# Products in 64-column halves, and seven products for eight in the third stage of a four-stage graph network

## The chip, the cores and the metric

The kernel runs on one core of a Trainium2 chip. The metric is the time of one execution on the device in microseconds (us). All data are float32.

## The reference

There are 32 graphs of 512 nodes with 128 features each, and each graph has a dense 512 x 512 weight matrix `adj`. Four residual stages follow one another; each normalises its input (layer norm and relu) and adds its result.

```python
h = relu(layernorm(x)); x = x + L0(h, adj)   # D^-1/2 (adj+I) D^-1/2 (h W) + b, leaky relu
h = relu(layernorm(x)); x = x + L1(h, adj)   # adj @ elu(.), adj^T @ elu(.), elu(.) -> W_upd, tanh
h = relu(layernorm(x)); x = x + L2(h, adj)   # four layers, see below
h = relu(layernorm(x)); x = x + L3(h, adj)   # tanh(adj @ msg), then a GRU cell
# a layer of L2; its inputs are f, f, [f, f1], [f, f1, f0] for i = 0..3
src_agg = l2norm_rows(adj)   @ (f @ ws + bs)
dst_agg = l2norm_cols(adj).T @ (f @ wd + bd)
f = tanh(concat([src_agg, f @ wn + bn, dst_agg]) @ wu + bu)
```

L2 is the "stage three" of the change, and the layers of L2 are counted from 0.

## The kernel before, in words

The host only lays out the inputs and hands over `adj` and its transpose. On the core, `program(b)` lists all operations of graph b, and every operation goes through `op(engine, us, emit, reads, writes)` with a planned duration: `t_mm`, `t_tt`, `t_act` and so on. Nothing is issued at that point. `Plan.order()` then plays the list through with these durations: each engine takes the ready operation with the earliest due time (`PERIOD` microseconds from graph to graph, less the planned work still behind it), and a tile of a limited kind waits for a slot. The kinds are PSUM banks (8) and SBUF slots of 2, 4 and 8 KB per partition, named `s2`, `s4` and `s8` (36, 5 and 10). What comes out is one fixed order per engine, in which several graphs are interleaved; it is issued as it stands, so an engine whose next operation is late waits for it. `kept_warm` puts idle products into planned gaps of TensorE.

Features are mostly held with 128 features (or 128 nodes) on the partitions and 512 columns in the free dimension. `a` and `aT` are the two forms of the matrix of a graph, four chunks of 128 x 512 each. A product is one `matmul` with 128 stationary columns (features, weights) and up to 512 moving ones; `mm` at L353 issues most of them, so that the tile names tell them apart. The profile shows two MATMUL and two LDWEIGHTS records for each.

The third stage works as follows. The squares of `a` and `aT` are summed on ScalarE, their inverse roots are made on POOL (L1077, `inv`), turned, sent to DRAM and spread over all partitions by SP (`rows`, L1088), and VectorE scales the columns of the eight chunks in place (L1096). Weights of the update are folded into the projections in `setup`. A layer then is: `paired_rows` (tile `sd`, four products of 256 columns, the bias added on VectorE at L791), one or two node products, and eight aggregation products of 512 columns, all into one PSUM bank (`ps_agg`), the tanh on ScalarE (L1136), ahead of it a sum on VectorE for layers 2 and 3 (L1135). Layer 1 is in `fifteen`: the two aggregations of the features themselves (eight products of 512 columns, `ps_agg<-aT,f1r` and `ps_agg<-a,f1r`), then fifteen products of 256 columns (L914) that serve layers 1, 2 and 3. The projection of layer 3 is in `seven` (L835): a two by two product of blocks in seven products, of 14 matmuls of 128 columns, with sums and differences on VectorE (L813).

Layer norms go through VectorE (`bn_stats`, L646), a power on POOL (L688, `sc`), `nb` on VectorE (L696), and four activations on ScalarE (L700, `h`). Transposes are made by VectorE in 32 x 32 blocks and a way through DRAM (`turned`, about a thousand transfers by SP), except in graphs 0, 1 and 31 (`at_ends`), where TensorE transposes 128 x 128 blocks (L733, L753, L876). POOL issues no transfers.

Of the kernel before, what the change touches and what calls it, by code (L numbers as in the profile page):

```python
# [18 lines left out]
P = 128  # L19
# [5 lines left out]
PERIOD = 37.0  # L25
# [6 lines left out]
GATES = 5 * D  # L32
FIFTEEN = GATES + 4 * D
T_COLS = FIFTEEN + 6 * D
# [65 lines left out]
class Plan:  # L100
# [65 lines left out]
    def lag(self, o, n):  # L166

        queued = o.engine == n.engine and o.engine in self.RESULT
        if queued:
            return o.us + self.RESULT[o.engine]  # L170
        return o.us + o.land + self.SIGNAL[o.engine] + self.LOAD * (n.engine == "PE")
# [110 lines left out]
def gnn_stack(  # L282
# [16 lines left out]
    plan = Plan(sb, psum, {"bank": 8, "s2": 36, "s4": 5, "s8": 10}, {"bank": 0, "s2": 4, "s4": 0, "s8": 0})  # L299
# [51 lines left out]

    def mm(ps, out_of, lhs, rhs, n, start, stop, reads, later=0.0):
        op("PE", t_mm(n), lambda: nc.tensor.matmul(out_of(ps.ap()), lhs(), rhs(), start=start, stop=stop),  # L353
           reads, [ps], later=later)

    LAST = [W_L2[3][0] + (2 * k + o) * D for k in (2, 0) for o in range(2)]
# [8 lines left out]
    def t15(k):  # L365
        return t_sb[:, FIFTEEN + k * D:FIFTEEN + (k + 1) * D]

    def setup():
# [35 lines left out]
        for i, (k, (proj, upd)) in enumerate(zip(L2_CHUNKS, RAW_L2, strict=True)):  # L404
            part = [0, 2] * k + [1] * k
            buf = raws[i][0]
            for lo in range(0, 3 * k, NC):
                n = min(NC, 3 * k - lo)
                ps = plan.bank(f"fold{i}_{lo}")
                for j in range(n):  # L410
                    mm(ps, lambda t, j=j: t[:, j * D:(j + 1) * D],
                       lambda i=i, c=proj + (lo + j) * D: block(i, c),
                       lambda i=i, c=upd + part[lo + j] * D: block(i, c), D, True, True, [buf])
                at = W_L2[i][0] + lo * D
                op("ACT", t_act(n * D), lambda ps=ps, n=n, at=at: nc.scalar.copy(
                    w_sb[:, at:at + n * D], ps.ap()[:, :n * D]), [ps], [(W2F, {i})])
# [16 lines left out]
            else:  # L433
                op("ACT", t_act(2 * D), lambda ps=ps, r=ROW_OF[i]: nc.scalar.copy(
                    rf_sb[:, r * 2 * D:(r + 1) * 2 * D], ps.ap()[:, :2 * D]), [ps], [RF])
        for at, (b11, b12, b21, b22), wbuf in ((0, LAST, (W2F, {3})), (GATES, BOTH, W3)):

# [10 lines left out]
        m, c = rf_sb, ROW_OF[3] * 2 * D  # L448
        op("DVE", t_tt(D), lambda: nc.vector.tensor_sub(t_sb[:, 4 * D:5 * D], m[:, c:c + D], m[:, c + D:c + 2 * D]), [RF], [(TS, {4})])
# [33 lines left out]
    def program(b):  # L483
# [13 lines left out]
        def gates(h3T, mT):  # L497
# [17 lines left out]
            def product(o, data, weight, wbuf, first):  # L515
                op("PE", t_mm(H), lambda: nc.tensor.matmul(o[0](), weight(), data[0](), start=first, stop=True, skip_group_check=True), [data[1], wbuf], [o[1]])  # L516

# [209 lines left out]
        def added_rows(x, m, quiet=False):  # L727

            o = buf("s2", rows_shape, "xr")
            if at_ends:  # L730
                ps = plan.bank("t")
                for c in range(NC):
                    op("PE", 0.109, lambda c=c: nc.tensor.transpose(ps.ap()[:, c * P:(c + 1) * P], m.ap()[:, c * P:(c + 1) * P], ident),  # L733
                       [m, ID], [(ps, {c})])
# [14 lines left out]
        def transposed(h, name):  # L749
            if at_ends:  # L750
                ps, hT = plan.bank("t"), buf("s2", name=name)
                for c in range(NC):
                    op("PE", 0.109, lambda c=c: nc.tensor.transpose(ps.ap()[:, c * P:(c + 1) * P], h.ap()[:, c, :], ident),  # L753
                       [(h, {c}), ID], [(ps, {c})])
# [24 lines left out]
        def paired_rows(nodes, wcols, wbuf, bias, bbuf, col):  # L779

            sd = buf("s4", (P, NC, 2 * D), "sd")
            for h in range(NC // 2):
                ps = plan.bank("sd")
                for j in range(2):
                    c = 2 * h + j
                    for k, nk in enumerate(nodes):
                        mm(ps, lambda t, j=j: t[:, j * 2 * D:(j + 1) * 2 * D],
                           lambda nk=nk, c=c: nk.ap()[:, c * P:(c + 1) * P],
                           lambda k=k: wt(wcols + k * 2 * D, 2 * D), 2 * D, k == 0, k == len(nodes) - 1, [nk, wbuf])
                part = (sd, set(range(4 * h, 4 * h + 4)))  # L790
                op("DVE", t_tt(N), lambda ps=ps, h=h: nc.vector.tensor_add(  # L791
                    sd.ap()[:, 2 * h:2 * h + 2, :], ps.ap().rearrange("p (j v) -> p j v", j=2),
                    along(bias, col, 2 * D, 2)), [ps, bbuf], [part])
            return sd

        def seven(x1, x2, dst, part, behind):

            at = 0  # L800
            (b11, b12, b21, b22), wbuf, (bias, bc), bbuf = LAST, (W2F, {3}), (rf_sb, ROW_OF[3] * 2 * D), RF
            H = N // 2
            s13, s24, ev, dv, xx = (buf("s2", (P, 2, H), k) for k in ("s13", "s24", "ev", "dv", "xx"))
            bank_a, bank_b, bank_c, bank_d = (plan.bank("seven") for _ in range(4))

            def half(m, k):
                return m.ap()[:, k * H:(k + 1) * H]

            def t(k):
                return t_sb[:, at + k * D:at + (k + 1) * D]  # L810

            def dve(o, a, b, reads, writes, sub=False, behind=()):
                op("DVE", t_tt(H), lambda: nc.vector.tensor_tensor(o(), a(), b(), op=ALU.subtract if sub else ALU.add), reads, writes, behind=behind)  # L813

            def place(k, o):
                return lambda: dst(k, o)

            def of(m, k):
                return lambda: m.ap()[:, k, :]

            def flat2(m, k):
                return lambda: m.ap()[:, k, :].rearrange("p (j v) -> p j v", j=2)

            def region(ps, k):
                return lambda: ps.ap()[:, k * H:(k + 1) * H]

            def region2(ps, k):
                return lambda: ps.ap()[:, k * H:(k + 1) * H].rearrange("p (j v) -> p j v", j=2)

            def along2(m, c):  # L830
                return lambda: m[:, None, c:c + D].to_broadcast([P, 2, D])

            def product(ps, k, lhs, rhs, reads, behind=()):
                for j in range(2):
                    op("PE", t_mm(D), lambda j=j: nc.tensor.matmul(  # L835
                        ps.ap()[:, k * H + j * D:k * H + (j + 1) * D], lhs()[:, j * P:(j + 1) * P], rhs(),
                        start=True, stop=True), reads, [ps], behind=behind)

            def pair(m):
                return lambda: m.ap().rearrange("p k (j v) -> p k j v", j=2)  # L840


            dve(of(s13, 1), lambda: half(x1, 0), lambda: half(x1, 1), [x1], [(s13, {1})], True, behind)
            product(bank_a, 0, lambda: half(x1, 0), lambda: wt(b11), [x1, wbuf], behind)
            product(bank_a, 1, of(s13, 1), lambda: t(2), [(s13, {1}), (TS, {at + 2})])
            dve(flat2(ev, 0), region2(bank_a, 0), along2(bias, bc + D), [bank_a, bbuf], [(ev, {0})])
            dve(of(ev, 1), region(bank_a, 1), of(ev, 0), [bank_a, (ev, {0})], [(ev, {1})])
            op("DVE", t_tt(N), lambda: nc.vector.tensor_add(
                pair(dv)(), pair(ev)(), t_sb[:, None, None, at + 4 * D:at + 5 * D].to_broadcast([P, 2, 2, D])), [ev, (TS, {at + 4})], [dv])

            product(bank_d, 0, lambda: half(x2, 0), lambda: wt(b21), [x2, wbuf])
            dve(of(s24, 0), lambda: half(x2, 1), of(s13, 1), [x2, (s13, {1})], [(s24, {0})], sub=True)
            dve(of(s13, 0), lambda: half(x1, 1), lambda: half(x2, 1), [x1, x2], [(s13, {0})])
            dve(of(s24, 1), lambda: half(x2, 0), of(s24, 0), [x2, (s24, {0})], [(s24, {1})], sub=True)
            product(bank_b, 0, of(s24, 0), lambda: t(1), [(s24, {0}), (TS, {at + 1})])
            product(bank_b, 1, of(s13, 0), lambda: t(0), [(s13, {0}), (TS, {at})])

            product(bank_c, 0, lambda: half(x2, 1), lambda: t(3), [x2, (TS, {at + 3}), bank_b])
            product(bank_c, 1, of(s24, 1), lambda: wt(b22), [(s24, {1}), wbuf])
            dve(place(0, 0), region2(bank_d, 0), flat2(dv, 0), [bank_d, dv], [part(0, 0)])  # L860
            op("DVE", t_tt(N), lambda: nc.vector.tensor_add(
                ev.ap(), bank_b.ap()[:, None, :H].to_broadcast([P, 2, H]), ev.ap()), [bank_b, ev], [ev])
            dve(of(xx, 0), region(bank_b, 0), of(dv, 1), [bank_b, dv], [(xx, {0})])
            dve(place(1, 1), region2(bank_b, 1), flat2(ev, 1), [bank_b, ev], [part(1, 1)])
            dve(place(1, 0), region2(bank_c, 0), flat2(xx, 0), [bank_c, (xx, {0})], [part(1, 0)])
            dve(of(xx, 1), region(bank_b, 1), of(ev, 0), [bank_b, ev], [(xx, {1})])
            dve(place(0, 1), region2(bank_c, 1), flat2(xx, 1), [bank_c, (xx, {1})], [part(0, 1)])

        def fifteen(f1, shares):


            H = N // 2
            if at_ends:
                pst, f1r = plan.bank("t"), buf("s2", rows_shape, "f1r")
                for c in range(NC):
                    op("PE", 0.109, lambda c=c: nc.tensor.transpose(pst.ap()[:, c * P:(c + 1) * P], f1.ap()[:, c * P:(c + 1) * P], ident),  # L876
                       [f1, ID], [(pst, {c})])
# [343 lines left out]
```

## Time and profile before

| what | value |
|---|---|
| time, median of 3 runs | 2275.66 us (2275.64 to 2276.08) |
| profiled execution: its time and span | 2275.95 us and 2274.2 us |
| granted TensorE clock | 1.0 |
| share of the span in which PE, PEld, DVE, ACT, POOL are busy | 100%, 58%, 71%, 48%, 10% |
| matmul records | 7608 |
| DMA: moved, mean rate, share of 16 engines of the main queue | 263.03 MB, 116 GB/s, 37.6% |

PE is TensorE's matmuls, PEld its weight loads, DVE is VectorE, ACT ScalarE, POOL GpSimd and SP SyncE, which here issues transfers. A busy time is the union of the instructions of an engine; matmuls overlap their successors, so for TensorE the distance from start to start says more than the length of a record. In a group of instructions the columns after the bar are busy time in us, mean length in ns, and the idle time of the engine just before.

### The profile page before, as it was taken

The page shows a single profiled execution, that of the slowest core. Times are in us where ns is not written, and L with a number is a line of the kernel's source. Part 1 is how long each engine was busy: PE and PEld are TensorE (multiplying, and loading weights), DVE is VectorE, ACT ScalarE, POOL GpSimd, SP SyncE. Part 2 cuts the span into 40 slices and gives each one's busy share as a digit, 9 for nine tenths or more (in the row PEclk, how much of TensorE's full clock was granted, in tenths as well). Part 3 has the DMA queues.
Part 4 walks back from the last instruction along what each step waited for, and adds up shares of the span by engine and source line. Part 5 has one row for each costly group of instructions (what it writes and reads, how often), then busy time and mean ns, then how long its engine had stood idle before and what let it go on. Part 6 is the DMA issues. An engine that isn't in the chain of part 4 may idle for free.

```text
span 2274.2 us, 25755 instructions
## 1 busy us (share of the span) xinstructions
PE 2263.3 (100%) x7608; PEld 1311.8 (58%) x7608; DVE 1607.0 (71%) x4346; ACT 1101.4 (48%) x2563; POOL 216.6 (10%) x203
## 2 busy tenths in 40 slices
PE   9999999999999999999999999999999999999999
PEld 6555565555565555555555655555555556555556
DVE  6756676767777777767777777777677777776655
ACT  7643554544445544455544455445555444552422
POOL 2100100100100100001001001000010010010000
PEclk9999999999999999999999999999999999999999
DMA  8032333444333443334443334443344333333212
GB/s 295 29 105 77 111 99 117 139 128 127 119 105 121 130 130 120 107 117 135 132 123 121 104 120 130 130 120 108 115 136 134 122 117 106 121 99 91 79 42 65
DMA packets 199052, 263.03 MB, mean 116 GB/s; under 512 B 25984, under 2 KB 130688, under 8 KB 198912
## 3 DMA queue, kind: packets, MB, share of 16 engines
q1 hardware_dynamic: 198624, 261.26, 37.6%
q8 instruction: 60, 0.98, 0.2%
q14 instruction: 80, 0.66, 0.1%
q10 hardware_dynamic: 288, 0.13, 0.0%
HBM read 199.18 MB, written 62.13 MB: 115 GB/s over the span
## 4 chain that ended last, share of the span: by engine, by line
PE 95%; DMA 2%; DVE 2%; ACT 0%; issue 0%; SPq 0%; POOL 0%; ACTq 0%; DVEq 0%; POOLq 0%
PE ps_agg L353 61%; PE ps_fifteen L914 9%; PE ps_sd L353 7%; PE ps_seven L835 4%; PE ps_seven L516 4%; PE ps_upd L353 3%; PE ps_gate L353 3%; PE ps_lin L353 1%; PE ps_msg L353 1%; PE ps_node L353 1%; DMA last<-turn_last 0%; DMA turned<-turn_turned 0%; DMA bounce<-invT 0%; DMA r_sb<-in_brow 0%; DMA turn_turned<-blk 0%; DMA rows<-bounce 0%
## 5 line engine op out<-in xcount | busy, mean ns | idle before, releaser
L353 PE MATMUL ps_agg<-a,sd 128*128 128x512 f32 x768 | 385.3, 593 | 0.0
L353 PE MATMUL ps_agg<-aT,sd 128*128 128x512 f32 x768 | 380.5, 593 | 0.4 <-DVE sd L791 0.2
L688 POOL TENSOR_TENSOR sc<-v,neg_half 128x4 f32<-128x4 f32 (+1 forms) x127 | 150.6, 1186 | 1710.5 <-DVE v L649 1603.5
L353 PEld LDWEIGHTS ps_agg<-aT,sd 128*128 128x128 f32 x768 | 136.6, 191 | 86.4 <-issue 77.5
L700 ACT ACTIVATE h<-xr,nb,sc 128x128 f32<-128x128 f32 x384 | 157.9, 482 | 49.1 <-DVE nb L696 49.1
L353 PEld LDWEIGHTS ps_agg<-a,sd 128*128 128x128 f32 x768 | 137.0, 191 | 62.0 <-issue 53.8
L353 PE MATMUL ps_sd<-w_sb,f 128*128 128x256 f32 x512 | 145.6, 380 | 0.9 <-ACT f L1112 0.9
L353 PEld LDWEIGHTS ps_sd<-w_sb,f 128*128 128x128 f32 x512 | 94.4, 190 | 77.6 <-issue 61.7
L1136 ACT ACTIVATE f<-c,cf_sb 128x512 f32<-128x512 f32 x64 | 46.2, 722 | 179.8 <-DVE c L1135 179.8
L353 PE MATMUL ps_agg<-f,w_sb 128*128 128x512 f32 x256 | 130.9, 593 | 0.1
L353 PE MATMUL ps_agg<-aT,f1r 128*128 128x512 f32 x256 | 130.7, 592 | 0.0
L353 PE MATMUL ps_agg<-a,f1r 128*128 128x512 f32 x256 | 130.7, 592 | 0.0
L353 PE MATMUL ps_agg<-aT,h 128*128 128x512 f32 (+2 forms) x260 | 128.7, 583 | 0.6 <-ACT h L673 0.6
L353 PE MATMUL ps_agg<-a,rep 128*128 128x512 f32 x256 | 125.5, 592 | 0.0
L353 PE MATMUL ps_agg<-aT,rep 128*128 128x512 f32 x256 | 121.6, 595 | 2.0 <-DVE rep L1049 1.8
L353 PE MATMUL ps_agg<-aT,msg 128*128 128x512 f32 (+1 forms) x264 | 116.7, 579 | 0.0
L791 DVE TENSOR_TENSOR sd<-ps_sd,rf_sb 128x512 f32<-128x512 f32 x128 | 87.9, 687 | 32.3 <-PE ps_sd L353 31.9
L1096 DVE TENSOR_TENSOR a<-a,rows 128x512 f32<-128x512 f32 x128 | 87.2, 687 | 16.7 <-PE ps_agg L353 16.1
L709 DVE STREAM_TRANSPOSE blk<-h 128x512 f32<-128x512 f32 x87 | 61.4, 706 | 51.4 <-ACT h L700 51.2
L1077 POOL TENSOR_TENSOR inv<-stat,neg_half 128x8 f32<-128x8 f32 x32 | 59.4, 1857 | 308.8 <-DVE stat L1076 287.9
L1096 DVE TENSOR_TENSOR aT<-aT,rows 128x512 f32<-128x512 f32 x128 | 86.4, 684 | 2.0 <-PE ps_agg L353 1.9
L1136 ACT ACTIVATE f<-ps_agg,cf_sb 128x512 f32<-128x512 f32 x32 | 22.0, 687 | 131.8 <-PE ps_agg L353 131.8
(229 smaller groups left out, 4424.6 us busy)
## 6 DMA issues: line engine op xcount, KB each, us to landing
aT<-in_adjt SPq DMA_DIRECT2D x124, 512.0 KB, 3.9
turn_turned<-blk SPq DMA_DIRECT2D x696, 64.0 KB, 1.8
turned<-turn_turned SPq DMA_DIRECT2D x174, 256.0 KB, 2.7
a<-in_adj SPq DMA_DIRECT2D x62, 512.0 KB, 7.5
rows<-bounce SPq DMA_DIRECT2D x32, 512.0 KB, 3.7
shares<-bounce SPq DMA_DIRECT2D x32, 512.0 KB, 4.4
x<-in_x SPq DMA_DIRECT2D x32, 256.0 KB, 2.7
out<-xr SPq DMA_DIRECT2D x31, 256.0 KB, 3.1
```

The costliest lines, as they stand in the source:

```text
L353: op("PE", t_mm(n), lambda: nc.tensor.matmul(out_of(ps.ap()), lhs(), rhs(), start=start, stop=stop), reads, [ps], later=later)
L516: op("PE", t_mm(H), lambda: nc.tensor.matmul(o[0](), weight(), data[0](), start=first, stop=True, skip_group_check=True), [data[1], wbuf], ...
L688: op("POOL", t_pow(n), lambda: nc.gpsimd.tensor_tensor(inv.ap()[:, :n], v8.ap()[:, :n], neg_half[:, :n], op=ALU.pow), [v8, NH], [(inv, {0})])
L700: op("ACT", t_act(D, 2), lambda c=c: nc.scalar.activation(h.ap()[:, c, :], xin.ap()[:, c, :], AF.Relu, bias=nb.ap()[:, c:c + 1], scale=inv ...
L709: op("DVE", t_tt(N), lambda: nc.vector.transpose(blk.ap().rearrange("p b (c r) -> p c b r", c=NC), m.ap().rearrange("p c (b s) -> p c b s" ...
L791: op("DVE", t_tt(N), lambda ps=ps, h=h: nc.vector.tensor_add(sd.ap()[:, 2 * h:2 * h + 2, :], ps.ap().rearrange("p (j v) -> p j v", j=2), a ...
L835: op("PE", t_mm(D), lambda j=j: nc.tensor.matmul(ps.ap()[:, k * H + j * D:k * H + (j + 1) * D], lhs()[:, j * P:(j + 1) * P], rhs(), start= ...
L914: op("PE", t_mm(H), lambda: nc.tensor.matmul(o[0](), weight(), data[0](), start=first, stop=True, skip_group_check=True), [data[1], wbuf], ...
L1077: roots = op("POOL", t_pow(2 * NC) + 0.4, lambda: nc.gpsimd.tensor_tensor(inv.ap()[:, :2 * NC], stat.ap(), neg_half, op=ALU.pow), [stat, N ...
L1096: op("DVE", t_tt(N), lambda m=m, c=c, s=s: nc.vector.tensor_mul(m.ap()[:, c, :], m.ap()[:, c, :], rows.ap()[:, s, :]), [(m, {c}), rows], [ ...
L1136: end = op("ACT", t_act(N, 1), lambda to=to, i=i, f_new=f_new: nc.scalar.activation(f_new.ap(), to.ap(), AF.Tanh, bias=cf_sb[:, i:i + 1]), ...
```

## The change

There are three parts. Every matmul of the kernel is issued as two, one for each half of the stationary columns, which write partitions 0 to 63 and 64 to 127 of PSUM (`by_halves`); the transposes on TensorE at the ends become products with the identity. In stage three the aggregations of layers 0, 2 and 3 (`features`) and of layer 1 (`edges`) are cut into two by two blocks: 64 features, two chunks of nodes, 256 columns. They take seven block products instead of eight, and two block products that write different halves of the partitions are issued side by side (`side_by_side`), each 256 columns wide. The sums of the blocks of the features are made on VectorE (`left_sums`), those of the matrices by copies on ScalarE and by transfers that POOL issues and that add to what is at their destination (`made_of`). `seven` is gone; layer 3 uses `paired_rows` with two inputs. Every second chunk of the scaled matrices, and of the projected features, has its sign turned. The weights of the projections and of the nodes are rearranged to match in `setup`.

The constants of the plan change too: `PERIOD`, the slots of `s2` and `s8`, and a new kind `s6` for the sums.

```diff
-PERIOD = 37.0
+PERIOD = 41.0
-    plan = Plan(sb, psum, {"bank": 8, "s2": 36, "s4": 5, "s8": 10}, {"bank": 0, "s2": 4, "s4": 0, "s8": 0})
+    plan = Plan(sb, psum, {"bank": 8, "s2": 31, "s4": 5, "s6": 4, "s8": 8}, {"bank": 0, "s2": 2, "s4": 0, "s6": 0, "s8": 0})
...
+    def by_halves(to, weight, data, start, stop):
+        for c in HALVES:
+            nc.tensor.matmul(to[c], weight[:, c], data, start=start, stop=stop, skip_group_check=True)
+
     def mm(ps, out_of, lhs, rhs, n, start, stop, reads, later=0.0):
-        op("PE", t_mm(n), lambda: nc.tensor.matmul(out_of(ps.ap()), lhs(), rhs(), start=start, stop=stop),
-           reads, [ps], later=later)
+        op("PE", t_mm(n), lambda: by_halves(out_of(ps.ap()), lhs(), rhs(), start, stop), reads, [ps], later=later)
+
+    def turn_on_pe(ps, part, columns, reads):
+        op("PE", t_mm(P), lambda: by_halves(ps.ap()[:, part * P:(part + 1) * P], columns(), ident, True, True), reads + [ID], [(ps, {part})])
...
-                    op("PE", 0.109, lambda c=c: nc.tensor.transpose(ps.ap()[:, c * P:(c + 1) * P], h.ap()[:, c, :], ident),
-                       [(h, {c}), ID], [(ps, {c})])
+                    turn_on_pe(ps, c, lambda c=c: h.ap()[:, c, :], [(h, {c})])
...
+        def made_of(m):
+            tm, even, odd = buf("s6", (P, 2, 3, H), "made"), {0, 2}, {1, 3}
...
+            def copied(k, src, reads):
+                op("ACT", t_act(N), lambda: nc.scalar.copy(t(k)(), src()), reads, [(tm, {k})])
+
+            def sent(o, x, reads, writes):
+                op("POOL", 1.95, lambda: nc.gpsimd.dma_start(o(), x(), accum_op=ALU.add), reads, writes).land = 5.5
+
+            copied(1, two(m, 0, 1), [(m, even)])
+            copied(0, two(m, 1, 1), [(m, odd)])
+            copied(2, two(m, 1, 0), [(m, odd)])
+            sent(two(m, 0, 1), two(m, 0, 0), [(m, even)], [(m, even)])
+            sent(t(1), two(m, 1, 1), [(m, odd), (tm, {1})], [(tm, {1})])
+            sent(t(0), two(m, 0, 1), [(m, even), (tm, {0})], [(tm, {0})])
+            sent(t(2), t(0), [(tm, {0, 2})], [(tm, {2})])
...
+        def side_by_side(lo, hi, begun):
+            for pair in zip(lo, hi, strict=True):
...
+                def emit(emits=emits):
+                    for to, lhs, rhs, start in emits:
+                        nc.tensor.matmul(to(), lhs(), rhs(), start=start, stop=True, skip_group_check=True)
+                op("PE", t_mm(H), emit, reads, writes)
+
+        def features(i, sd, nodes, made, f_new, more):
...
+            left_sums(H, lambda h, k: lambda: sd.ap().rearrange("p (q k) (h v) -> p q k h v", k=2, h=2)[:, :, k, h, :],
...
+            lo = products(A, 1, q4) + products(C, 5, q4) + node(C, 1, 1) + products(A, 2, q4) + node(A, 0, 0) + products(C, 3, q2)
+            hi = products(Bh, 6, q4) + node(Dh, 2, 1) + products(Dh, 3, (2, 3)) + products(Bh, 7, q4)
+            second = len(hi)
+            hi += products(Bh, 4, q4) + node(Bh, 1, 0)
...
+            side_by_side(lo[:4], hi[:4], begun)
+            copy(p1_lo, A)
+            add(d, p1_lo, Bh)
...
+            side_by_side(lo[4:second], hi[4:second], begun)
...
+            add(quarter[1, 1], e, C)
+            side_by_side(lo[second:], hi[second:], begun)
...
+        def edges(f1r, made, ge):
...
+            left_sums(P, part, f1r, st, lambda k: lambda: st.ap()[:, k])
...
+            products(0, 1)
...
-            ge = buf("s4", (P, 2, N), "ge")
-            for k, m in enumerate((aT, a)):
-                ps = plan.bank("agg")
-                for c in range(NC):
-                    mm(ps, lambda t: t, lambda c=c: chunk(c), lambda c=c, m=m: m.ap()[:, c, :], N, c == 0, c == NC - 1, [f1r, (m, {c})])
+            ge = buf("s4", (P, 2, N), "ge")
+            edges(f1r, made, ge)
...
-            if i == 3:
-                sd = buf("s4", (P, NC, 2 * D), "sd")
-                seven(f0, f, *of_halves(sd), [third_started])
+            if i == 3:
+                sd = paired_rows([f0, f], [wsd + 4 * D, wsd], (W2F, {i}), rf_sb, RF, ROW_OF[i] * 2 * D)
+                nodes.append((f0, wn + 2 * D, 3))
+            end = features(i, sd, nodes, made, f_new, later[i - 2] if i > 1 else None)
```

The sums of the results in `features` (`add`, `copy` and the tanh) run on VectorE and ScalarE: for layer 0 six sums of 256 columns and one copy, for layers 2 and 3 eight sums of 256, one of 512 and two copies each; in `edges` two sums and six more, all of 256, and three copies.

## The prediction

> **What bounds the kernel now.** I read the page first: the busy line and the chain of waits.
>
> ```profile
> PE 2263.3 (100%) x7608; PEld 1311.8 (58%) x7608; DVE 1607.0 (71%) x4346; ACT 1101.4 (48%) x2563; POOL 216.6 (10%) x203
> PE 95%; DMA 2%; DVE 2%; ACT 0%; issue 0%; SPq 0%; POOL 0%; ACTq 0%; DVEq 0%; POOLq 0%
> ```
>
> TensorE is busy for the whole span and 95% of the chain lies on it. A busy PE is not yet a PE at its rate, so next I read the chain in order of time, where each piece runs from start to start.
>
> ```profile
> 335.49 10.30 PE ps_agg L353 x24
> 404.87 10.30 PE ps_agg L353 x24
> 474.24 10.30 PE ps_agg L353 x24
> ...
> 2163.97 1.73 PE ps_fifteen L914 x8
> ...
> 2207.42 0.89 PE ps_seven L835 x8
> ```
>
> Two records make one float32 product, so a product takes 10.30/12 = 0.858 us with 512 moving columns, 1.73/4 = 0.4325 with 256 and 0.89/4 = 0.2225 with 128. The same run of twelve comes back every 69.37 us: that is the time of one graph. The groups by shape give the number of products (records / 2 / 32 graphs).
>
> ```profile
> L353 PE MATMUL ps_agg<-a,sd 128*128 128x512 f32 x768 | 385.3, 593 | 0.0
> L353 PE MATMUL ps_agg<-aT,sd 128*128 128x512 f32 x768 | 380.5, 593 | 0.4 <-DVE sd L791 0.2
> ...
> L353 PE MATMUL ps_agg<-f,w_sb 128*128 128x512 f32 x256 | 130.9, 593 | 0.1
> L353 PE MATMUL ps_agg<-aT,f1r 128*128 128x512 f32 x256 | 130.7, 592 | 0.0
> L353 PE MATMUL ps_agg<-a,f1r 128*128 128x512 f32 x256 | 130.7, 592 | 0.0
> ...
> L835 PE MATMUL ps_seven<-t_sb,s 128*128 128x128 f32 x384 | 63.2, 274 | 0.0
> ```
>
> Over all groups a graph has 58 products of 512, 34 of 256 and 22 of 128 columns: 58 x 0.858 + 34 x 0.4325 + 22 x 0.2225 = 69.4 us, the whole period. No engine but TensorE sets it: a column less streamed is time saved, as long as nothing else becomes late. The next engine is VectorE.
>
> ```profile
> 900.00:969.60 69.60, 69.60 (x230) 40.05 (x229) 50.84 (x139) 34.34 (x80) 6.62 (x6) 1.00 0.40 126
> ```
>
> That window (PE, PEld, DVE, ACT, POOL, clock, DMA share, GB/s) is one graph: DVE 50.8 us of 69.6, ACT 34.3, POOL 6.6.
>
> **What the Trainium skill says.** "TensorEngine Tiling (Array Packing)", Key Properties: a matmul of at most 64 stationary columns uses a column tile, tiles load weights and multiply in parallel, and a change of the tiling mode drains the array. No run here has a column tile; with every product halved there is no change of mode. "TensorE: Matmul & The Clock Gate", LDWEIGHTS: a load takes columns/1.2 ns, 107 ns for 128. The trace agrees: six loads in a row start 22.24 - 21.57 = 0.67 us apart in all, 0.112 each.
>
> ```profile
> 21.57 0.75 PEld L353 LDWEIGHTS ps_foldb<-c_sb,raw 128*128 128x128 f32 x6
> 22.24 0.19 PEld L353 LDWEIGHTS ps_foldb<-raw,c_sb 128*128 128x128 f32 x1
> ```
>
> "SBUF — State Buffer", Who interferes with whom: descriptors of a transfer issued by GpSimd wait while VectorE is in a two-port mode; no transfer is issued there before, so no trace shows it.
>
> **The change part by part.** *Halves.* Each product becomes two of 64 stationary columns, on the same 512, 256 or 128 moving columns. I take the pair at the price of one whole product: two different tiles, and 4 loads of 64 columns (an estimate of 53 ns each from the page) instead of 2 of 128, the same load time. The bounds are a little below nothing (what a product takes beyond its columns, 2 x 0.4325 - 0.858 = 0.007 us, if tiles hide it: under 1 us a graph) and twice the time (no overlap).
>
> *Seven for eight.* Layers 0, 2 and 3 of stage three had 8 aggregation products of 512 each and 1, 1 and 2 node products, 28 in all; they become 14 pairs of 256 each and two pairs for each node input: 16, 16 and 18. The two aggregations of layer 1 (8 of 512) become 14 pairs of 256. Layer 3's projection, `seven` (14 of 128), becomes 8 of 256. Before: 36 x 0.858 + 14 x 0.2225 = 34.0 us. After: (50 + 14 + 8) x 0.4325 = 31.1 us. The saving is 2.86 us a graph, **91.5 us** over 32, all of it on the path; the graph is then 66.5 us of TensorE. At both ends 80 transposes, 0.108 us each from start to start (25.03 to 25.46 for four), become identity products of 0.2225: **+9 us**, in stretches where TensorE is also full.
>
> *VectorE.* Its rate is read from start to start:
>
> ```profile
> 1103.20 0.69 DVE L1096 TENSOR_TENSOR a<-a,rows 128x512 f32<-128x512 f32 x1
> 1103.80 0.69 DVE L1096 TENSOR_TENSOR aT<-aT,rows 128x512 f32<-128x512 f32 x1
> ...
> 1115.07 0.42 DVE L908 TENSOR_TENSOR xy<-xy,ge 128x256 f32<-128x256 f32 x1
> 1115.53 0.42 DVE L908 TENSOR_TENSOR xy<-xy,f 128x256 f32<-128x256 f32 x1
> 1115.87 0.42 DVE L908 TENSOR_TENSOR q<-ge 128x256 f32<-128x256 f32 x1
> ```
>
> 0.60 us for 512 columns, 0.34 for 256 (0.46 where it needs the one before it), 0.20 for 128 as an estimate on that line. Removed: 12 of 256 and 2 of 512 in `seven`, the two sums of L1135 and four biased copies, all of 512: 12 x 0.34 + 8 x 0.60 = 8.9 us. Added: 12 biased copies, 12 left sums, 22 sums of results (6, 8, 8) and 8 in layer 1, all of 256, two of 512, four of 128, one small: 54 x 0.34 + 2 x 0.60 + 4 x 0.20 + 0.1 = 20.5 us. Net +11.6, so 62.4 us a graph; at the full lengths (0.69, 0.42, 0.28), as where each needs the last, +14.7 and 65.5. VectorE goes from 73% of the period to 94% or more of 66.5 us. Its idle 18.8 us a graph were what let it answer at once; with 1 to 4 left, TensorE will wait for sums now and then. No row prices this. Bounds: nothing, and 2.86 us a graph, at which the gain is gone (beyond it lies a rival below). I take a third, 1 us a graph: **+32 us**.
>
> *ScalarE.* Six copies of 512 (0.62 each), five more of 256 (0.37) in the layers and the tanh of layer 0 in three parts (+1.0), layer 1 +0.6: about +7 us, 41 of 66.5. Cost nothing, hidden beside TensorE; the copies come long before use, as shown next.
>
> *Transfers that add.* Eight a graph of 256 KB, issued by POOL, in two chains of up to three. "DMA: Bandwidth & Descriptors", Anatomy of one DMA, prices one at 2.0 us + bytes/436e3, 2.6 us as an estimate, and says nothing of adding; the plan books 1.95 us on POOL and 5.5 to land. A chain of three so takes 8 to 22 us. The cover: a graph's matrices are scaled until 1110.4 (the last L1096 at 1109.70), and its first features are back from DRAM only at 1136.68, its first projection at 1138.37: 28 us. So nothing on the path while the landing stays under some 8 us; past that, layer 0 waits and another graph's products must fill in. POOL rises from 6.6 to about 22 us a graph. Behind a send that waits for the one before stand the powers of L688 and L1077; the nb of L696 on VectorE, the h on ScalarE and a transpose wait for those. The DMA share of 0.40 gains 2 MB beside 8.2 (263 MB / 32), under 0.2 even if each byte counts twice: room. SP's queue issues what it did.
>
> *Buffers.* Of the 8 KB slots 8 are left of 10. A matrix lives about 270 us (issued near 967, last used near 1237), so two take 270 x 2 / 69.4 = 7.8 slots, with the reloaded one on top: the loads must come later. They are some 50 us ahead of the first use (the diagonal copy at 1017.1), so I cost this at nothing; with the cover gone, a load's 3.9 to 7.5 us would stand ahead of a graph's start. The 2 KB slots fall from 36 to 31, where `seven` alone held five. The other constants of the plan only change order.
>
> **The sum.** The profiled execution took 2275.95 us (span 2274.2, so 1.75 around it; 0.3 over the median of 2275.66): 2275.95 - 91.5 + 9 + 32 = 2225.5, said as **2226 us**.
>
> **The rivals.** *VectorE takes over as the bound (slower).* Place: the six sums behind each pair of banks, in order, with 62.4 to 65.5 us of work. If it can be kept busy only 92% of the time, the period is 65.5 / 0.92 = 71.2 us: +1.8 x 32 + 9 = 2343 us. It decides below 65.5 / 69.1 = 95% (69.1 = 69.37 - 9/32). For it: the 73% leave no precedent, and its order is fixed from planned durations. Against: the 62.4, and three to four graphs under way for TensorE to turn to.
>
> *Loads set the pace (slower).* A load of 64 columns might take as long as one of 128: 4 x 0.112 = 0.448 us a product against 0.4325 and 0.2225. That adds 106 x 0.0155 + 8 x 0.2255 = 3.45 us a graph: 2226 + 110 = 2336 us. It eats the whole saving from about 0.105 us a load. Against: the page's columns/1.2.
>
> *The halves don't overlap: the change doesn't do what it says.* Each product at twice its time: 133 us a graph, 2275.95 + 32 x (133 - 69.37) = 4312 us. For it: no column tile in this trace. Against: the skill ("TensorE: Matmul & The Clock Gate", Part 3, three column tiles ran 2.38 times as fast, though not said for float32).
>
> **How the numbers follow.** Forecast 0.55, its own range 2175 to 2265 (waits of 0 to 2.2 us a graph, and a little for overheads that tiles hide); VectorE 0.22, 2250 to 2360, a fifth of it still faster; loads 0.12, 2300 to 2420; no overlap 0.08; below 2175 0.03. A range of 2175 to 2360 holds about eight in ten. Faster 0.55 + 0.03 + 0.05 = 0.63; same 0.04; slower 0.33, where 0.2% is about what a measurement of this kernel can tell from no change.
>
> **What would show it.** Right: the pairs of one bank 0.43 us from start to start; the period near 67.5 us; DVE over 60 us a graph; TensorE's gaps short and ended by DVE sums; the sends landing in under 8 us. Wrong: products of 256 columns at 0.448 or more (loads) or 0.86 (no overlap); PE under 96% with DVE near 100%; gaps ended by a DMA of `made` or by POOL's powers, the landing or the queue I costed at nothing.

## The result and the profile after

The changed kernel takes **2499.6 us** (median of 4 runs, 2495.1 to 2502.0) where the kernel before takes 2275.9 beside it: 1.098 times as long, 95% interval 1.0961 to 1.0999. The forecast was 2226. The page of after, busy line and chain of waits:

```profile
PE 2311.3 (92%) x18376; PEld 1369.1 (55%) x18376; DVE 2025.3 (81%) x5657; ACT 1298.7 (52%) x3105; POOL 529.5 (21%) x459
PE 35%; DVE 26%; DMA 17%; issue 10%; ACT 5%; POOL 4%; SPq 2%; ACTq 0%; DVEq 0%; POOLq 0%
```

TensorE, 100% busy and 95% of the chain before, now idles 8% of the span and is a third of the chain. VectorE is no bound either; 17% of the chain are transfers, which were 2%. The queues of the DMA engines in after (packets, MB, share of all 16 engines' time):

```profile
q1 hardware_dynamic: 198624, 261.26, 35.2%
q0 software_dynamic: 69632, 67.13, 17.7%
```

The second line is new. Its 67 MB are a quarter of the other queue's bytes and take half of its time. The timeline of TensorE in after, at the same place of two neighbouring graphs (start, length, group, and in brackets the idle time before it and what ended that):

```profile
1009.30 0.65 PE L356 MATMUL ps_fifteen<-xy,w_sb 128*64 128x256 f32 x4 [2.72 <-DVE yx L1066]
...
1015.51 1.09 PE L356 MATMUL ps_msg<-w_sb,hT 128*64 128x128 f32 x16 [1.87 <-ACT hT L779]
...
1085.86 0.65 PE L356 MATMUL ps_fifteen<-xy,w_sb 128*64 128x256 f32 x4 [3.62 <-DVE yx L1066]
1086.34 1.02 PE L356 MATMUL ps_fifteen<-xy,t_sb 128*64 128x256 f32 x4
1087.14 0.64 PE L356 MATMUL ps_lin<-w_sb,agg 128*64 128x128 f32 x4
```

The period is 76.6 us here (1085.86 - 1009.30), where before had 69.37. TensorE stops for microseconds in stage three's layer 1 (`fifteen`), for a sum of VectorE. What VectorE did meanwhile, from its timeline in after:

```profile
1005.20 0.42 DVE L1066 TENSOR_TENSOR xy<-xy,f 128x256 f32<-128x256 f32 x1
1008.22 0.69 DVE L760 TENSOR_TENSOR xr<-turned,xr 128x512 f32<-128x512 f32 x1 [2.60 <-DMA turned<-turn_turned]
1008.83 0.42 DVE L1066 TENSOR_TENSOR yx<-ps_fifteen,pe 128x256 f32<-128x256 f32 x1
```

It waited 2.6 us for a turned block on its way back from DRAM, and the sum that TensorE needs came behind that. Over the whole run, the waits of VectorE for turned blocks in after (us in total, times, longest):

```profile
DVE xr L760 <- DMA turned<-turn_turned: 134.3, 56, 6.0
```

and in before:

```profile
DVE xr L738 <- DMA turned<-turn_turned: 27.6, 33, 3.9
```

The largest of TensorE's own waits in after is the one seen in the timeline:

```profile
PE ps_fifteen L356 <- DVE yx L1066: 76.5, 26, 5.8
```

The chain of after in order of time says what else is long:

```profile
992.29 9.67 DMA a<-in_adj
...
1005.28 2.92 DMA turned<-turn_turned
```

This matrix load takes 9.67 us, and the 13 loads on the chain take 9.1 to 10.1. A chain picks long transfers, so this is no fair comparison with the middle value before, 7.5 us.

A measure used below is the **late starts** of a kernel. I walk through TensorE's records from 400 to 2100 us, give each its length from start to start (a pair of halves 0.858, 0.4325 or 0.2225 us, as the prediction read them), and add up by how much they begin later than that asks for. It is 3 us for before and about 220 for after. The lengths are those at the full clock, so a product that runs at a lower clock makes the next one late too. The same lengths times all records give TensorE's work in the whole run: 2251.5 us before, 2179.0 after. The forecast's 91.5 - 9 = 82.5 us of saved work are there, less 10 us for 46 more warming products a run (`ps_idle`) that the order puts into gaps. The saved work is real; the late starts swallow it and more.

### The profile page after: what moved, and what is told of

Same layout as the page of the kernel before. It is cut to its first block, busy times and chain, and to the rows that moved or that the text cites. A ratio compares the mean times of both kernels' runs of the same rounds, so it can differ in the third digit from the quotient of the medians.

```text
span 2499.7 us, 50580 instructions
## 1 busy us (share of the span) xinstructions
PE 2311.3 (92%) x18376; PEld 1369.1 (55%) x18376; DVE 2025.3 (81%) x5657; ACT 1298.7 (52%) x3105; POOL 529.5 (21%) x459
## 3 DMA queue, kind: packets, MB, share of 16 engines
q0 software_dynamic: 69632, 67.13, 17.7%
## 4 chain that ended last, share of the span: by engine, by line
PE 35%; DVE 26%; DMA 17%; issue 10%; ACT 5%; POOL 4%; SPq 2%; ACTq 0%; DVEq 0%; POOLq 0%
PE ps_ab L892 9%; PE ps_sd L356 6%; DMA turned<-turn_turned 6%; PE ps_agg L356 5%; DMA a<-in_adj 5%; PE ps_cd L892 5%; DMA turn_turned<-blk 5%; POOL sc L711 4%; DVE blk L732 3%; DVE c L833 3%; PE ps_fifteen L356 3%; PE ps_seven L356 2%; SPq L741 2%; ACT h L723 2%; DVE bn L669 1%
## 5 line engine op out<-in xcount | busy, mean ns | idle before, releaser
L892 PE MATMUL ps_ab<-made,st 128*64 128x256 f32 x1536 | 390.3, 380 | 0.3 <-DVE p L833 0.2
L356 PE MATMUL ps_sd<-w_sb,f 128*64 128x256 f32 x2048 | 272.1, 388 | 26.1 <-DVE sd L819 13.7
L892 PE MATMUL ps_ab<-aT,sd 128*64 128x256 f32 x768 | 228.6, 385 | 1.3 <-DVE c L833 1.1
L892 PE MATMUL ps_ab<-a,sd 128*64 128x256 f32 x768 | 224.3, 380 | 0.0
L892 PEld LDWEIGHTS ps_ab<-made,st 128*64 128x64 f32 x1536 | 206.4, 137 | 25.2 <-DVE p L833 6.7
L356 PEld LDWEIGHTS ps_sd<-w_sb,f 128*64 128x64 f32 x2048 | 155.8, 140 | 110.7 <-PE ps_ab L892 23.4
L892 PE MATMUL ps_cd<-aT,st 128*64 128x256 f32 x768 | 216.1, 381 | 0.2
L892 PE MATMUL ps_cd<-a,st 128*64 128x256 f32 x768 | 210.7, 379 | 0.0
L892 PE MATMUL ps_ab<-made,sd 128*64 128x256 f32 x768 | 206.5, 386 | 0.0
L356 PE MATMUL ps_agg<-a,rep 128*64 128x512 f32 x512 | 177.5, 592 | 0.0
L760 DVE TENSOR_TENSOR xr<-turned,xr 128x512 f32<-128x512 f32 x58 | 40.1, 692 | 134.4 <-DMA turned<-turn_turned 134.3
```

What stands on the lines that cost most here:

```text
L356: nc.tensor.matmul(to[c], weight[:, c], data, start=start, stop=stop, skip_group_check=True)
L760: tt(o, lambda: nc.vector.tensor_add(o.ap().rearrange("p c (a r) -> p c a r", a=NC), turned_cols(t), x.ap().rearrange("p c (a r) -> p c a ...
L892: nc.tensor.matmul(to(), lhs(), rhs(), start=start, stop=True, skip_group_check=True)
```

## The experiments

The causes to tell apart are (1) the adding transfers, by their data and landing (1a) or by POOL's time to issue them (1b); (2) the fewer slots; (3) VectorE, by its load or by its chains of sums. Times stand beside a run of before on the same chip (2272 to 2276 us), ratios have 95% intervals.

### Halves alone

```diff
-        op("PE", t_mm(n), lambda: nc.tensor.matmul(out_of(ps.ap()), lhs(), rhs(), ...
+        op("PE", t_mm(n), lambda: by_halves(out_of(ps.ap()), lhs(), rhs(), start, stop), ...
```

> The kernel before, with every product issued as two halves of 64 stationary columns and the 80 transposes at the ends as products, and nothing else. If the halves are free, 2276 + 9 = about 2285 us. If column tiles cost something in the long run (loads, issue), 2340 us and up.

Measured 2277.6 us, ratio 1.0029 (1.0018 to 1.0040): +5.6 us, the transposes as products included. The timeline of TensorE in this kernel:

```profile
1000.81 1.03 PE L356 MATMUL ps_agg<-a,sd 128*64 128x512 f32 x4
1001.67 0.60 PE L356 MATMUL ps_fifteen<-ge,w_sb 128*64 128x256 f32 x4
1002.10 0.60 PE L356 MATMUL ps_seven<-hT,w_sb 128*64 128x256 f32 x4
```

Four half records, one pair, take 0.86 us with 512 columns and 0.43 with 256, as the whole products did. Halves cost nothing.

### After without the adding transfers

```diff
-            sent(two(m, 0, 1), two(m, 0, 0), [(m, even)], [(m, even)])
-            ... (all four of a matrix)
```

> The changed kernel without its eight adding transfers a graph (the sums of the matrices are left out, their copies on ScalarE, all sums on VectorE and the slots stay). Theory 1, the adding transfers delay the other transfers and POOL: most of the loss goes, 2230 to 2320 us. Theory 2, fewer slots make the loads late: 2430 us or more stays. Theory 3, VectorE has too much work: 2430 us or more stays.

Measured 2314.2 us, ratio 1.0185 (1.0170 to 1.0200). Without the transfers, and with a new order, 185 us are gone; it is still no gain.

### Before with the transfers, and before with the slots

```diff
+            sent(spare_t(0), two(m, 0, 0), [(m, {0, 2})], [(SPARE, {0})])
+            ... (four a matrix, into a tile that nobody reads)
```

> The kernel before, with eight adding transfers a graph of the same size and in the same chains put on POOL after the scaling, into a spare tile that nobody reads (33 slots of 2 KB for 36, to make room). Theory 1: 2350 to 2500 us. Theories 2 and 3: 2276 to 2290 us.

Measured 2365.2 us, ratio 1.0409 (1.0394 to 1.0425): 93 us although no product waits for the sums. The order is a new one here, with three slots of 2 KB fewer; what these two cost was not measured apart.

```diff
-PERIOD = 37.0
+PERIOD = 41.0
...
-"s2": 36, "s4": 5, "s8": 10}
+"s2": 31, "s4": 5, "s8": 8}
```

> The kernel before with the slots of the changed one (31 of 2 KB, 8 of 8 KB) and its PERIOD of 41, and nothing else. Theory 2: 2350 us or more, with ScalarE waiting for the loads of a. Theories 1 and 3: 2276 to 2300 us.

Measured 2312.1 us, ratio 1.0171 (1.0148 to 1.0194): the slots and the other period together cost before 40 us. It was neither the 2350 us of theory 2 nor the 2276 to 2300 of the others.

### Thin transfers

```diff
-nc.gpsimd.dma_start(o(), x(), accum_op=ALU.add)
+nc.gpsimd.dma_start(o()[:8], x()[:8], accum_op=ALU.add)
```

> The changed kernel with the same order on every engine and the same eight adding transfers and waits, but each moves the first 8 of 128 partitions only (so most of the sums of the matrices are left out). Theory 1a, what costs is the data that the adding transfers move through the DMA engines and their long landing: most of the 185 us goes, 2310 to 2350 us. Theory 1b, what costs is that POOL issues them in its queue, 1.2 us each, with powers behind: 2430 us or more.

Measured 2305.6 us, ratio 1.0138 (1.0123 to 1.0153). Order, instructions and POOL's queue are those of after, only the data are fewer, and **194 us** are gone. That is 1a and not 1b: POOL still issues all 256 transfers, though in less time (it is busy for 444.3 us in place of 529.5). VectorE's waits for turned blocks fall below those of before (12.8 us in 24 waits), the period is 70.1 us, the late starts are 85 us. TensorE's wait for `yx` is gone too:

```profile
PE ps_fifteen L356 <- DVE yx L1066: 3.1, 5, 1.2
```

A rival remains, which the prediction had named: a transfer that waits for the one before it holds up POOL's queue, and the powers of the layer norms stand behind it. VectorE's waits for these powers settle it, in after and in thin_sends:

```profile
DVE nb L719 <- POOL sc L711: 33.1, 31, 1.2
```

```profile
DVE nb L719 <- POOL sc L711: 32.7, 29, 1.2
```

They are the same, and none is longer than 1.2 us.

### The sums on GpSimd

```diff
-            sent(t(1), two(m, 1, 1), [(m, odd), (tm, {1})], [(tm, {1})])
+            sum_on("POOL", t(1), two(m, 0, 1), two(m, 1, 1), [m], [(tm, {1})])
```

> The changed kernel with the sums of the matrices made by GpSimd itself, four tensor additions of 512 columns for each matrix, straight into the tile; no adding transfers and no copies on ScalarE. Theory 1a: 2250 to 2330 us, as without the transfers. A rival, GpSimd's additions read the memory that VectorE's two-input sums read and slow them: VectorE's sums get longer and the time stays over 2350 us.

Measured 2465.9 us, ratio 1.0841 (1.0825 to 1.0857): no transfers, no copies on ScalarE, and hardly better. VectorE's groups in this kernel:

```profile
L1201 DVE TENSOR_TENSOR node<-zn,en 128x512 f32<-128x512 f32 x32 | 48.5, 1517 | 0.1
L1200 DVE TENSOR_SCALAR en<-en 128x512 f32<-128x512 f32 x32 | 40.2, 1256 | 1.3 <-ACT en L1197 1.3
L817 DVE TENSOR_TENSOR sd<-ps_sd,rf_sb 128x256 f32<-128x256 f32 x192 | 78.2, 407 | 51.7 <-PE ps_sd L356 51.7
```

and the same three in after:

```profile
L1200 DVE TENSOR_TENSOR node<-zn,en 128x512 f32<-128x512 f32 x32 | 21.8, 683 | 0.0
L1199 DVE TENSOR_SCALAR en<-en 128x512 f32<-128x512 f32 x32 | 13.4, 419 | 0.0
L817 DVE TENSOR_TENSOR sd<-ps_sd,rf_sb 128x256 f32<-128x256 f32 x192 | 78.6, 409 | 60.3 <-PE ps_sd L356 60.0
```

`node` and `en`, from SBUF to SBUF, take 1517 and 1256 ns in place of 683 and 419; `sd`, which reads one input from PSUM, takes what it took. VectorE's busy time rises by 147 us (2172.6 for 2025.3). The Trainium skill's "SBUF — State Buffer", Who interferes with whom, says so of `node`: VectorE shares a pair of ports with GpSimd, and an operation with both inputs in SBUF contends with one of GpSimd that reads SBUF. The late starts are 195 us; the largest group of them, 91, is in layer 1 (`ps_b`).

### Slots back, and fewer sums on VectorE

`no_sends_slots` gives the version without transfers its slots back ("s2" 33, "s8" 10); its products read the matrix in place of the sums.

```diff
-"s2": 31, "s4": 5, "s6": 4, "s8": 8}
+"s2": 33, "s4": 5, "s8": 10}
...
-                return (lambda: tm.ap()[:, pair, j, :]), (tm, {j})
+                return (lambda: m.ap()[:, c, h * H:(h + 1) * H]), (m, {c})
```

> The changed kernel without adding transfers, whose products read the matrix itself instead of the sums (left out), the copies going to one spare tile; the room goes back to slots: 33 of 2 KB and 10 of 8 KB. Theory 2 for the rest of the loss, too few slots: 2314 falls to 2200 to 2260 us. Theory 3, VectorE: 2300 us or more stays.

Measured 2329.9 us, ratio 1.0247 (1.0230 to 1.0264), not under 2314: more slots gain nothing there, so theory 2 doesn't explain what is left. (The order is a new one, and all graphs' copies go to one tile, so what slots alone are worth there was not measured.)

`no_left` keeps the order of after and doesn't issue the 16 left sums a graph.

```diff
-            summed(n, place(0), part(1, 1), part(1, 0), ALU.subtract, of(), [(st, {0})])
-            ... (four lines)
+                op("DVE", us, lambda: None, reads, writes)
```

> The changed kernel in the same order, with the 16 left sums a graph on VectorE not issued (the products read the blocks themselves, so these sums are left out), 4.9 us a graph less of VectorE. Theory 3, VectorE has too much work: 2350 to 2430 us. Theory 1: 2460 us or more, since the transfers stay.

Measured 2503.9 us, ratio 1.1008 (1.0992 to 1.1024): 140 us less of VectorE (1885.7), and no faster.

`thin_no_left` makes both edits, this one and the thin transfers'.

> The kernel after in its own order, with two things left out: the adding transfers move 8 of 128 partitions, and the 16 left sums a graph on VectorE (4.9 us a graph) are not issued. It asks what the thin transfers left over: they take 2306 us, and between 400 and 2100 us TensorE's products begin in all 85 us later than their lengths ask for, 3.5 us a graph. Theory A, VectorE's load: with 90% of its time taken it answers late, so with 4.9 us less a graph the waits fall to 1 us a graph and the time to about 2306 - 2.5 x 32 = 2226 us. Theory B, the length of the chains of sums and the order alone: the time stays within 12 us of 2306. The left sums alone changed nothing with the whole transfers (2504 against 2500), where late transfers ended the waits.

Measured 2304.3 us, ratio 1.0136 (1.0118 to 1.0154). VectorE's share of the stretch from 800 to 1200 us is 83% (333.8 of 400) where it was 90%, the late starts are 85 us as in thin_sends. Less load on VectorE brings nothing, with whole transfers or with thin ones.

### How the transfers cost

`unread`: in the order of after, all transfers with all bytes, and no product reads what they make.

```diff
-                return (lambda: tm.ap()[:, pair, j, :]), (tm, {j})
+                return (lambda: m.ap()[:, c, h * H:(h + 1) * H]), (tm, {j})
```

> The kernel after in its own order. All eight adding transfers are issued with all their bytes, but no product reads what they make: the products read the matrix itself instead of the sums (so the sums are left out of the result), and the transfer that adds within the matrix adds into a spare tile. Theory 1, traffic: the transfers slow the loads and the turning transfers, and these hold up the queues: the time stays within 30 us of 2500. Theory 2, lateness of the sums themselves: products wait for transfers that land late, so without that wait it falls towards the thin transfers' 2306, under 2360. Between them both have a share.

Measured 2516.0 us, ratio 1.1064 (1.1038 to 1.1090). No product waits for the sums, and the time is that of after or a little over: it is the traffic, not the lateness of the sums.

`half_sends`: 64 of 128 partitions.

```diff
-nc.gpsimd.dma_start(o(), x(), accum_op=ALU.add)
+nc.gpsimd.dma_start(o()[:64], x()[:64], accum_op=ALU.add)
```

> The kernel after in its own order, the adding transfers moving 64 of 128 partitions (the other half of each sum is left out). With 8 partitions it took 2306 us, with 128 it took 2500. If the cost goes with the bytes it is 2306 + 194 x 56 / 120 = 2397 us. If the order has slack for transfers up to some length and only what lands later than that costs, it is under 2345 us.

Measured 2422.9 us, ratio 1.0658 (1.0636 to 1.0680), 26 us over the figure by bytes. The order has no slack that would hide the first half.

`booked`: one number of the plan.

```diff
-writes).land = 5.5
+writes).land = 7.5
```

> The kernel after with one number of its plan changed: an adding transfer is booked with 7.5 us to land instead of 5.5 (the trace shows 4.4 to 9.5), so the order is another. If the loss came from an order made for too short a landing, at least 60 us of it come back: 2440 us or less. If it comes from the traffic, which is the same, it stays between 2470 and 2530 us.

Measured 2510.6 us, ratio 1.1044 (1.1025 to 1.1062): this order, made for a longer landing, is no better.

`plain_sends`: the same bytes copied instead of added.

```diff
-nc.gpsimd.dma_start(o(), x(), accum_op=ALU.add)
+nc.gpsimd.dma_start(o(), x())
```

> The kernel after in its own order, its eight transfers a graph with all their bytes, but they copy and don't add (the sums are left out: a matrix block replaces them). If the adding is what costs, the software queue's share of the DMA engines falls from 17.7% to some 9%, which is what its 67 MB would take at the rate of the other queue (261 MB in 35.2%), and the time to that of the transfers of half the bytes, 2423 us, or less. If each transfer costs by its bytes, added or not, the time stays within 30 us of 2500.

Measured 2372.2 us, ratio 1.0432 (1.0417 to 1.0448): two thirds of the 194 us are the adding. The software queue of this kernel:

```profile
q0 software_dynamic: 20480, 67.13, 8.1%
```

The same 67.13 MB, in 20480 packets for 69632, take less than half of the time on the engines. Put together (time on the engines is the queue's share times the span):

| kernel | software queue, us of all 16 engines | VectorE waits for turned blocks, us | time, us | over thin, per us of the queue |
|---|---|---|---|---|
| thin_sends | 60 | 12.8 | 2305.6 | |
| plain_sends | 192 | 59.0 | 2372.2 | 0.51 |
| half_sends | 286 | 86.4 | 2422.9 | 0.52 |
| after | 442 | 134.3 | 2499.6 | 0.51 |
| unread | 451 | 153.2 | 2516.0 | 0.54 |

All five issue their work in one order. The time follows neither bytes nor the number of transfers: plain_sends has as many of both as after. It rises with the time on the DMA engines, by about half a microsecond for each.

The even half microsecond is no constant, though. The mean granted clock is 0.999 in thin_sends and plain_sends, 0.987 in half_sends, 0.982 in after and 0.972 in unread. Times the span that is work lost to the clock of at most 2, 2, 32, 45 and 70 us, an estimate that takes TensorE as busy in the slow stretches. Without it the last column reads 0.50, 0.39, 0.40 and 0.36. So some 43 of the 194 us are the clock, which falls after TensorE's longer waits (the last section shows one), and the rest are waits. In before's order (before_sends, 19.2% of 2365.3 us) 454 us on the engines come with 93 us, 0.2 for each. Why that order loses less wasn't tried.

### The chain of sums

`thin_short` is thin_sends with shorter sums of results in layers 2 and 3.

```diff
-                added(o[0], x[0], y[0], [x[1], y[1]], [o[1]])
+                if more:
+                    added(*((lambda a=a: a[0]()[:, :Q]) for a in (o, x, y)), [x[1], y[1]], [o[1]])
```

> The thin transfers again (8 of 128 partitions, order of the kernel after), and in layers 2 and 3 the eight sums of results add 128 of their 256 columns only (the other half of each is left out): 16 sums a graph, each some 0.13 us shorter, on the way from one product's bank to the next. Theory B, the chain of sums behind each pair of banks sets when TensorE may go on: its waits fall in these two of four stages, and the time goes from 2306 to 2285 us or less. Rival, the waits come from the order as a whole and move elsewhere when one link is shorter: within 12 us of 2306.

The kernel that ran adds 64 of the 256 columns of each sum, not 128 as the expectation says. Measured **2263.7 us**, ratio 0.9957 (0.9943 to 0.9971). The sums of results in thin_sends, and in thin_short:

```profile
L833 DVE TENSOR_TENSOR c<-c,ps_ab 64x256 f32<-64x256 f32 x192 | 80.2, 418 | 12.2 <-PE ps_ab L892 8.3
```

```profile
L833 DVE TENSOR_TENSOR c<-c,ps_ab 64x64 f32<-64x64 f32 x192 | 42.0, 219 | 15.5 <-PE ps_ab L892 11.5
```

16 sums a graph, each 0.2 us shorter, are 3.2 us of VectorE and bring 42 us, 1.3 a graph; the 4.9 us of left sums, made well ahead of their use, brought 1 us. Late starts fall from 85 to 49, and those of the next products (`ps_sd<-w_sb,f`, `ps_ab<-f,w_sb`) from 32 to 13. A bank is written up to three times in a layer and each time TensorE must wait for the sum that reads it. The length of this chain counts, not VectorE's load.

### Is it the head of the queue?

The timeline suggests that a late block does harm because it stands ahead of other sums. Three kernels with all of after's work move only that (their expectations call layer 1 of stage three "stage two"): `behind_xr` the sum xr by up to two places in VectorE's queue, `behind` also the copies hT and the row sums sq on ScalarE, `behind_8` xr and all that needs it by eight places.

```diff
+            if o in self.slow:
+                held.append([o, self.PAST])
```

> The kernel after, all of its work and transfers, with one kind of instruction moved: in VectorE's queue the sum that takes back a turned block from DRAM (xr L760, 58 of them, the head of the queue for 134 us of waits) is issued up to two VectorE instructions later, past those that don't need it. In the trace of after it stands ahead of a sum of stage two (yx) that TensorE's products wait for: 75 us of late starts at that product. Theory, head of the queue: these sums come in time and a part of it comes back, 30 us or more: 2470 or less. Rival, the blocks are needed so soon that the wait only moves to what reads them, or the late transfers bind elsewhere: 2485 to 2515.

> The same for all three kinds of instructions that stand at a queue's head and wait for a transfer: xr on VectorE, the copies of turned blocks (hT L779) and the row sums of a newly loaded matrix (sq L1143) on ScalarE, each up to two instructions of its engine later. Theory, head of the queue: more comes back than from xr alone: 2450 or less. Rival, as above: 2485 to 2515.

> The kernel after with all its work; each sum of a turned block (xr) stands eight instructions further back in VectorE's queue, and what needs it goes back with it. In behind_xr it had moved by two at most, by one on average, and the wait went to the next sums behind it (vs L1086 in place of yx L1066). Theory, head of the queue: with eight sums let past (some 3 us of work against waits of 2.4 us on average) TensorE's products of stage two come in time: 2450 or less. Rival: the turned blocks are themselves needed at once, so what is won at stage two is lost where the normalized features are awaited: 2485 or more.

Measured 2521.9 us (ratio 1.1091, 1.1073 to 1.1110), 2507.1 (1.1029, 1.1010 to 1.1047) and 2532.6 (1.1130, 1.1111 to 1.1148): each no better than after. TensorE's waits in behind_8 (us in total, times, longest) are:

```profile
PE ps_fifteen L381 <- DVE q L1092: 76.1, 26, 3.2
PE ps_msg L381 <- ACT hT L805: 63.0, 24, 4.0
```

VectorE no longer waits for turned blocks, but TensorE waits as long for another sum of layer 1, and three times as long for the features that come out of xr (21 us in after). None of the three moves bears out my theory of the queue's head. They fit the rival: the blocks are late for their own readers, and the wait goes where one puts it. All three move by a fixed number of places, so they also put off blocks that were in time; a move of the late ones alone wasn't tried.

## Why the prediction was wrong, point by point

- **Halves at the price of whole products: right**, +5.6 us with the transposes where I had +9. The rivals "loads set the pace" and "no overlap" are out. (By its own figures the first eats the whole saving from 0.111 us a load, not 0.105.)
- **Seven for eight saves 2.86 us a graph of TensorE: right as work**, not as time.
- **VectorE's waits, 1 us a graph: too small, by 80 us in all.** thin_sends has what the forecast supposed, transfers that weigh little, and takes 2305.6 us. My sum without waits was 2275.95 - 91.5 + 9 = 2193.5, so 112 us are left for waits, 3.5 a graph, over the 2.86 at which I said the gain is gone. The late starts say the same: 85 us between 400 and 2100 us are 3.5 for each period of 70.1. VectorE's work was as forecast (63.3 us a graph, 2025.3 / 32), and so was the place, the sums behind each pair of banks. But the rival's reason, an engine that can't be filled beyond 92%, is not it: at 83% the waits are the same. 1.3 us of the 3.5 went with shorter sums in layers 2 and 3. What makes the rest wasn't tried; the thin transfers themselves, 60 us on the DMA engines, may have a part in it.
- **Transfers that add, at nothing: the step that failed.** They cost 194 us of the 274 by which the forecast missed. The figures in it held: eight transfers, 2 MB a graph, and a DMA share of 0.54 in the stretch from 800 to 1200 us, under the 0.60 I allowed. My condition was that "the landing stays under some 8 us", and the landings are 4.4 to 9.5 us by group, so one group of five breaks it. But I asked only whether the sums come in time for layer 0, and that is not where the cost lies: unread, in which no product waits for them, is no faster, and in the trace of after TensorE waits nowhere for a transfer of `made`, a sign that I had named. "Room" on the engines was the wrong test. The matrix loads and the six turning trips a graph (174 over 29 graphs) use the same engines, VectorE and then TensorE wait for them, and I never priced their lateness.
- **POOL's queue: right that it is free**, as the equal waits for its powers show. A send takes it 1.2 us (313 us more for 256), not 1.95.
- **Buffers at nothing: wrong in before's setting** (40 us with the period), with no gain from more slots in the version without transfers.
- **ScalarE at nothing: right as work**, 40.6 us a graph (1298.7 / 32) for 41 forecast. No run tried its cost alone.
- **The rivals: no range holds 2500 us.** The two slow ones ended at 2360 and 2420, no overlap stood at 4312, and none was about the transfers.

The sum closes by its making: 2193.5 + 112 + 194 = 2499.5. That the traffic's 194 and the other 112 are separate costs is shown by thin_sends alone.

Which of the delayed transfers, loads or turning trips, carries most of the 194 stays open, but the traces say something. On the chain of after the writes of a block to DRAM (`turn_turned<-blk`) have a median of 3.5 us, on that of thin_sends 2.0; the reads back (`turned<-turn_turned`) have 3.0 and 2.9. Of the turning trip it is the write that gets longer. The loads of `a` on the chain take 9.5 us in after and as much, 9.4, in plain_sends, which is 127 us faster, so a longer load alone doesn't make the difference between these two. No version with the seven products and all the work beats before.

## What to carry to other kernels

Free time on the DMA engines was no cover for new traffic here: ask which transfers lie between dependent stages, and count what the new engine time adds to them. When an edit splits a product into pieces with sums between, price the chain from bank to sum to bank, not the load of the engine that sums. A wait that stands at the head of a queue is not proof that the queue is at fault: move it and see whether the time moves.

## What the runs showed that I had not expected

- An adding transfer within SBUF holds the DMA engines 2.3 times as long as a copy of the same bytes (442 against 192 us for 67.13 MB), in 3.4 times as many packets. One of 256 KB landed in 4.4 to 9.5 us by group.
- After an idle stretch of 3.62 us TensorE runs slower: a group with 256 columns takes 0.80 us from its start to the next group's (1086.34 to 1087.14) where 0.43 is usual, and the trace shows a granted clock of 0.5 from 1086.4 to 1089.8. In after there are 22 such spells before the end of the run, each 3.41 or 6.83 us long and each beside an idle stretch of 2.25 to 7.17 us (some stretches of over 2.25 us have none). thin_sends has one, at its start. So waits cost more than their length.
- Beside GpSimd's additions VectorE's smallest operations stretch as much as the large: `nb`, 128x4, took 399 ns for 159.
